# A max-pooling layer's scratch images and group statistics rearranged: one horizontal image, a ring of four pools, statistics on ScalarE

## The chip, the cores and the metric

The kernel runs on one core of a Trainium2 chip. The metric is the device time of one execution in microseconds, as the median of several runs. Five engines work side by side, each with its own in-order instruction queue: TensorE (PE in the profile, its weight loads PEld), VectorE (DVE), ScalarE (ACT), GpSimd (POOL) and SyncE (SP), which here only issues DMAs. They wait for each other through semaphores.

## The reference

The program is four layers applied in turn to two images of 512 channels and 64 x 64 pixels, fp32; each layer adds its result to its input after a group normalization (32 groups of 16 channels). The change is in the third layer, which is a mixture of max pools:

```python
gap = jnp.mean(x, axis=(2, 3))
hmid = jax.nn.relu(jnp.einsum('bc,ec->be', gap, w1) + b1)
score = jnp.einsum('be,ce->bc', hmid, w2) + b2
s = jax.nn.relu(score)
q_s = jnp.clip(jnp.floor(jax.lax.stop_gradient(s)), 0, n_k - 2).astype(jnp.int32)
q_b = q_s + 1
pools = jnp.stack([_maxpool_same(x, k) for k in KERNELS], axis=2)   # KERNELS = 1, 3, 5, 7, 9, 11, 13
...
return frac_b * b_out + frac_s * s_out + x                         # x = x + layer(_gn(x))
```

For each channel, two neighbouring pool sizes are weighted by how far a score lies between two whole numbers. The score comes from the normalized channel means through two small matrices.

## The kernel before, in words

An image lies in SBUF as four chunks of 128 channels (one per partition) x 4096 pixels: `X`, 64 KB per partition. A second buffer of the same size, `Y`, is scratch in this layer. Two such buffers, 128 KB of each partition, live through the whole program.

The layers follow one another. The kernel is written as a data flow, and a framework places each instruction in its engine's queue when the program is built, so that queues don't keep the order of the source: in VectorE's queue the first pooling operations of the third layer stand ahead of the statistics that the source names first. The order is fixed in the built program. Dependent instructions, on one engine or on several, are ordered by semaphores.

The third layer of `Net` (the class that runs; `General` is a fallback behind a condition) has two parts.

`pool_weights` (L1139, calling L637) makes the weights. `self.mv` holds mean and variance per channel, left by the second layer's last step (L1022, L1025). `group_stats` (L75) turns them into group statistics: a small matmul with `self.grp` averages the means over 16 channels (L87), ScalarE negates the result (L89), VectorE centres, squares and adds the channel variances (L92 to L94), a second matmul averages them (L96), VectorE adds the epsilon (L97), and GpSimd raises to the power -1/2 (L99). Then come the normalized means `gap` (L643, L644), two matmuls (L647, L653) with a ReLU between on ScalarE (L650), and some 34 VectorE instructions of 128 x 4 elements (L656 to L680) which make the seven weights per channel `wts`, the factor `c0` of the image itself and the shift `d0`. All of L656 to L665, and the seven triples L670 to L672 that share one tile `t`, depend on each other in turn.

`pool_chunk` (L1140) works on one chunk `cc` of four. A pool of size 2j+1 is made from that of size 2j-1 by a 3 x 3 maximum, horizontal and then vertical. `spread_max` (L683) takes the maximum of the two outer neighbours for all but the edges on VectorE (L692, 3968 elements) and copies the two edge columns or rows on ScalarE (L693). For j = 1 the centre is added by a second maximum each (L1161, L1163). So a chunk has 14 large VectorE operations: 4 for j = 1 and 2 for each of j = 2 to 6. The horizontal results h and the pools p alternate between two images each: h in `Y[:, 0]` and `Y[:, 1]`, p in `Y[:, 2]` and `Y[:, 3]`. Here h1, p1 and so on mean the images of step j.

The weighting is done by TensorE: `add` scales the identity matrix by a column of weights on ScalarE (`dg`, three buffers, L1151) and multiplies each of the eight 512-pixel blocks by it, accumulating in eight PSUM banks (L1153). Seven such sums, of the image and of p1 to p6, make the chunk's result. A pool's image can be overwritten when its sum has read it: p3 takes p1's image, p4 that of p2. ScalarE then moves the eight banks to `X` with the shift (L1183, and L1175 in the last chunk), and statistics for the fourth layer are taken (L1188 to L1196, or L1176 and L1177).

Of the kernel before, what the change touches and what calls it, by code (L numbers as in the profile page):

```python
# [8 lines left out]
F32 = mybir.dt.float32  # L9
I32 = mybir.dt.int32  # L10
AF = mybir.ActivationFunctionType
ALU = mybir.AluOpType
# [3 lines left out]
P = 128  # L16
C = 512
KC = C // P
W = 64
N = W * W  # L20
TB = 512
# [20 lines left out]
def bcast(ap, axis, n):  # L42

    a = ap.unsqueeze(axis)
    shape = list(a.shape)
    shape[axis] = n
    return a.to_broadcast(shape)
# [10 lines left out]
class General:  # L58
# [578 lines left out]
    def pool_weights(self, X, w1, w2, sp, pp, mv=None):  # L637


        nc, vec = self.nc, self.vec  # L640
        nmean, rstd, mv = self.group_stats(X, sp, pp, mv)
        gap = sp.tile([P, KC], F32, name="gap")
        nc.vector.tensor_tensor(gap, mv[:, :, 0], nmean, ALU.add)  # L643
        nc.vector.tensor_tensor(gap, gap, rstd, ALU.mult)  # L644
        ps = pp.tile([P, TB], F32, name="mm")
        for kc in range(KC):
            nc.tensor.matmul(ps[:32, :1], w1[:, kc, :], gap[:, kc:kc + 1], start=(kc == 0),  # L647
                             stop=(kc == KC - 1))
        mid = sp.tile([32, 1], F32, name="mid")
        nc.scalar.activation(mid, ps[:32, :1], AF.Relu, bias=vec[:32, V_B1:V_B1 + 1])  # L650
        ps = pp.tile([P, TB], F32, name="mm")
        for oc in range(KC):
            nc.tensor.matmul(ps[:, oc:oc + 1], w2[:, oc * P:(oc + 1) * P], mid, start=True,  # L653
                             stop=True)
        s, q, t, fb, fs = (sp.tile([P, KC], F32, name=f"pw_{n}") for n in ("s", "q", "t", "fb", "fs"))
        nc.vector.tensor_tensor(s, ps[:, :KC], vec[:, V_B2:V_B2 + KC], ALU.add)  # L656
        nc.vector.tensor_scalar(s, s, 0.0, None, ALU.max)

        nc.vector.tensor_scalar(q, s, 8.0, None, ALU.min)
        qi = sp.tile([P, KC], I32, name="pw_qi")  # L660
        nc.vector.tensor_copy(qi, q)
        nc.vector.tensor_copy(q, qi)
        nc.vector.tensor_tensor(t, q, s, ALU.is_gt)
        nc.vector.tensor_tensor(q, q, t, ALU.subtract)
        nc.vector.tensor_scalar(q, q, 5.0, None, ALU.min)  # L665
        nc.vector.tensor_tensor(fb, s, q, ALU.subtract)
        nc.vector.scalar_tensor_tensor(fs, q, 1.0, s, ALU.add, ALU.subtract)
        wts = sp.tile([P, 7, KC], F32, name="pw_w")
        for j in range(7):
            nc.vector.scalar_tensor_tensor(wts[:, j], q, float(j), fs, ALU.is_equal, ALU.mult)  # L670
            nc.vector.scalar_tensor_tensor(t, q, float(j - 1), fb, ALU.is_equal, ALU.mult)
            nc.vector.tensor_tensor(wts[:, j], wts[:, j], t, ALU.add)  # L672
        c0 = sp.tile([P, KC], F32, name="pw_c0")
        d0 = sp.tile([P, KC], F32, name="pw_d0")
        nc.vector.tensor_tensor(d0, fs, fb, ALU.add)
        nc.vector.scalar_tensor_tensor(d0, d0, 1.0, nmean, ALU.add, ALU.mult)
        nc.vector.tensor_tensor(d0, d0, rstd, ALU.mult)
        nc.vector.tensor_tensor(wts, wts, bcast(rstd, 1, 7), ALU.mult)
        nc.vector.tensor_tensor(c0, wts[:, 0], rstd, ALU.add)
        nc.vector.tensor_scalar(c0, c0, 1.0, None, ALU.add)  # L680
        return c0, d0, wts
# [13 lines left out]
    def pool_chunk(self, X, Y, cc, c0, d0, wts, sp, ppa):  # L695

        nc = self.nc
        x2 = X[:, cc, :]
        img = x2.rearrange("p (y x) -> p y x", x=W)
        tmp = [Y[:, i, :].rearrange("p (y x) -> p y x", x=W) for i in range(KC)]  # L700
        accs = []
        for j in range(1, 7):
            h, p = tmp[j % 2], tmp[2 + j % 2]
            if j == 1:
                self.spread_max(h, img, 2)
                nc.vector.tensor_tensor(h, h, img, ALU.max)
                self.spread_max(p, h, 1)
                nc.vector.tensor_tensor(p, p, h, ALU.max)
                for b in range(NB):
                    xx = x2[:, b * TB:(b + 1) * TB]  # L710
                    nc.scalar.activation(xx, xx, AF.Identity, bias=d0[:, cc:cc + 1],
                                         scale=c0[:, cc:cc + 1])
            else:

                self.spread_max(h, tmp[2 + (j - 1) % 2], 2)
                self.spread_max(p, h, 1)
            dg = sp.tile([P, P], F32, name="dg", bufs=3)
            nc.vector.tensor_scalar(dg, self.ident, wts[:, j, cc:cc + 1], None, ALU.mult)
            p2 = Y[:, 2 + j % 2, :]
            for b in range(NB):  # L720
                if j == 1:
                    acc = ppa.tile([P, TB], F32, name="acc")
                    accs.append(acc)
                nc.tensor.matmul(accs[b], dg, p2[:, b * TB:(b + 1) * TB], start=(j == 1),
                                 stop=(j == 6))
        for b in range(NB):
            xx = x2[:, b * TB:(b + 1) * TB]
            nc.vector.tensor_tensor(xx, xx, accs[b], ALU.add)
# [199 lines left out]
class Net(General):  # L928
# [206 lines left out]
        return w  # L1135

    def pool_weights(self, X, w1, w2, sp, pp):
        return super().pool_weights(X, w1, w2, sp, pp, self.mv)

    def pool_chunk(self, X, Y, cc, c0, d0, wts, sp, ppa):  # L1140


        nc = self.nc
        x2 = X[:, cc, :]
        img = x2.rearrange("p (y x) -> p y x", x=W)
        tmp = [Y[:, i, :].rearrange("p (y x) -> p y x", x=W) for i in range(KC)]
        accs = [ppa.tile([P, TB], F32, name="acc") for b in range(NB)]

        def add(w, src, j):
            dg = sp.tile([P, P], F32, name="dg", bufs=3)  # L1150
            nc.scalar.activation(dg, self.ident, AF.Copy, scale=w)  # L1151
            for b in range(NB):
                nc.tensor.matmul(accs[b], dg, src[:, b * TB:(b + 1) * TB], start=(j == 0),  # L1153
                                 stop=(j == 6))

        add(c0[:, cc:cc + 1], x2, 0)
        for j in range(1, 7):
            h, p = tmp[j % 2], tmp[2 + j % 2]
            if j == 1:
                self.spread_max(h, img, 2)  # L1160
                nc.vector.tensor_tensor(h, h, img, ALU.max)  # L1161
                self.spread_max(p, h, 1)
                nc.vector.tensor_tensor(p, p, h, ALU.max)  # L1163
            else:

                self.spread_max(h, tmp[2 + (j - 1) % 2], 2)
                self.spread_max(p, h, 1)
            add(wts[:, j, cc:cc + 1], Y[:, 2 + j % 2, :], j)
        mv = self.mv[:, cc]
        if cc == KC - 1:  # L1170

            st = sp.tile([P, NB, 6], F32, name="pool_st")
            for b in range(NB):
                xx = x2[:, b * TB:(b + 1) * TB]
                nc.scalar.activation(xx, accs[b], AF.Identity, bias=d0[:, cc:cc + 1])  # L1175
                nc.vector.bn_stats(st[:, b, :], xx)  # L1176
            nc.vector.bn_aggr(mv, st.rearrange("p b s -> p (b s)"))  # L1177
            return
        sums = sp.tile([P, 2, NB], F32, name="pool_sums", bufs=2)
        shift = sp.tile([P, 1], F32, name="pool_shift", bufs=2)  # L1180
        for b in range(NB):
            xx = x2[:, b * TB:(b + 1) * TB]
            nc.scalar.activation(xx, accs[b], AF.Identity, bias=d0[:, cc:cc + 1],  # L1183
                                 accum_out=sums[:, 0, b:b + 1])
            if b == 0:
                nc.scalar.mul(shift, sums[:, 0, 0:1], -1.0 / TB)
            junk = sp.tile([P, TB], F32, name="pool_sq", bufs=2)
            nc.scalar.activation(junk, xx, AF.Square, bias=shift, accum_out=sums[:, 1, b:b + 1])  # L1188
        total = sp.tile([P, 2], F32, name="pool_total", bufs=2)
        nc.vector.tensor_reduce(total, sums, AX.X, ALU.add)  # L1190
        nc.vector.tensor_scalar(total, total, 1.0 / N, None, ALU.mult)
        mean, var = mv[:, 0:1], mv[:, 1:2]
        nc.vector.tensor_copy(mean, total[:, 0:1])
        nc.vector.tensor_tensor(shift, shift, mean, ALU.add)
        nc.vector.tensor_tensor(shift, shift, shift, ALU.mult)
        nc.vector.tensor_tensor(var, total[:, 1:2], shift, ALU.subtract)  # L1196
# [1187 lines left out]
```

## Time and profile before

| | us |
|---|---|
| median of 3 runs | 5740.13 (5734.53 to 5741.96) |
| the profiled execution, its own time | 5741.67 |
| its span, from the first to the last instruction | 5739.9 |
| mean granted TensorE clock | 0.963 |
| TensorE busy | 5451.3 (95%) |
| VectorE busy | 3020.0 (53%) |
| ScalarE busy | 1496.6 (26%) |
| GpSimd busy | 2032.2 (35%) |
| third layer, first image: first L692 to last channel statistics (L1177) | 1693.69 to 1975.16 |
| third layer, second image: first L692 | 4540.70 |

A line of a group gives the source line, engine, operation, the names of what it writes and reads, the shape, and after the bar the busy time in us, the mean of one in ns, the idle time ahead of it and what ended it. A line of the timeline gives start and duration in us, then engine, line, operation and shape, and in brackets the idle time of that engine just before, with the instruction that ended it. A line of waits gives who waited for whom, the us in total, how often, and the longest. Ends of matmuls and spans on POOL are approximate.

### The profile page before, as it was taken

The numbers are of one execution on the slowest core, as the hardware profiler recorded it, in microseconds if no ns is written. First come the engines' busy times: TensorE is split into PE (matmuls) and PEld (weight loads), VectorE is DVE, ScalarE is ACT, GpSimd is POOL, SyncE is SP. The second block draws the span as 40 slices with busy tenths as digits, with TensorE's granted clock in tenths as the row PEclk, the third lists the DMA queues.
The fourth block names the chain that finished last, engine by engine and source line by source line (L and its number), as shares of the span: only waits on it lengthen the run. The fifth ranks groups of instructions, "written<-read, shape, count | busy, mean of one in ns | idle before, by whom it ended". The sixth has DMA issues, their size and how long they took to land.

```text
span 5739.9 us, 52308 instructions
## 1 busy us (share of the span) xinstructions
PE 5451.3 (95%) x20443; PEld 2351.5 (41%) x20443; DVE 3020.0 (53%) x3408; ACT 1496.6 (26%) x2837; POOL 2032.2 (35%) x1518
## 2 busy tenths in 40 slices
PE   7899999999988899999998999999999788999999
PEld 4333333455333344544343333334553234445443
DVE  3245655644678733554432555566456696334444
ACT  1233333114212233222212333330242122332221
POOL 0145666510320045443401565664002200454443
PEclk9899999999998999999998999999999899999999
DMA  3000001100000000101010000011000000000000
GB/s 138 0 10 15 13 15 34 59 24 8 16 1 0 1 1 1 74 15 37 30 54 2 8 15 17 15 34 55 24 24 1 1 0 1 1 1 16 21 15 23
DMA packets 52435, 118.15 MB, mean 21 GB/s; under 512 B 4882, under 2 KB 17938, under 8 KB 50132
## 3 DMA queue, kind: packets, MB, share of 16 engines
q1 hardware_dynamic: 52180, 114.72, 5.7%
q8 instruction: 163, 2.67, 0.2%
q14 instruction: 92, 0.75, 0.0%
HBM read 74.86 MB, written 39.85 MB: 20 GB/s over the span
## 4 chain that ended last, share of the span: by engine, by line
PE 66%; DVE 9%; issue 3%; ACT 1%; POOL 1%; DMA 0%; DVEq 0%; ACTq 0%; POOLq 0%; SPq 0%
PE mm L133 19%; DVE big L692 6%; PE mm L1330 4%; PE mm L1615 4%; PE mm L1370 4%; PE mm L547 4%; PE mm L1932 2%; PE mm L1226 2%; PE mm L1410 2%; PE psO L1242 2%; PE psO L1602 2%; PE mm L2203 2%; PE mm L1631 2%; PE mm L2129 1%; PE tap L2097 1%
## 5 line engine op out<-in xcount | busy, mean ns | idle before, releaser
L133 PE MATMUL mm<-big,w 128*128 128x512 f32 x2560 | 1203.6, 615 | 0.0
L2214 POOL TENSOR_TENSOR late<-late,big 128x512 f32<-128x512 f32 x576 | 718.9, 1282 | 374.9 <-DVE big L2209 374.9
L133 PEld LDWEIGHTS mm<-big,w 128*128 128x128 f32 x2560 | 471.5, 194 | 699.0 <-issue 636.5
L1153 PE MATMUL acc<-big,dg 128*128 128x512 f32 x896 | 407.7, 614 | 79.3 <-DVE big L692 51.1
L2209 DVE TENSOR_TENSOR big<-big,mm 128x512 f32<-128x512 f32 x576 | 364.1, 682 | 194.7 <-PE mm L2203 178.0
L692 DVE TENSOR_TENSOR big<-big 128x3968 f32<-128x3968 f32 x96 | 410.8, 4289 | 38.2 <-PE acc L1153 32.7
L1232 POOL TENSOR_TENSOR total<-prob 128x512 f32<-128x512 f32 x128 | 159.8, 1270 | 761.1 <-ACT prob L1229 761.1
L1584 POOL TENSOR_SCALAR qf_sum<-qf,ksum_ratio 128x512 f32<-128x512 f32 x128 | 199.1, 1565 | 552.1 <-ACT qf L1634 351.5
L1405 POOL TENSOR_TENSOR big<-big 128x512 f32<-128x512 f32 x224 | 278.0, 1273 | 234.9 <-ACT big L1396 234.9
L1609 DVE RECIPROCAL k<-psD 128x512 f32<-128x512 f32 x64 | 214.9, 3358 | 185.0 <-PE psD L1606 185.0
L1153 PEld LDWEIGHTS acc<-big,dg 128*128 128x128 f32 x896 | 173.9, 197 | 311.6 <-issue 283.4
L2144 POOL TENSOR_TENSOR late<-late 128x512 f32<-128x512 f32 x128 | 160.2, 1273 | 383.4 <-ACT late L2133 360.4
L2203 PE MATMUL mm<-late,tapb 18*128 18x512 f32 x1152 | 278.2, 635 | 4.4 <-DVE big L2209 3.3
L1396 ACT ACTIVATE big<-mm,ed 128x256 f32<-128x256 f32 x512 | 194.4, 490 | 276.6 <-DVE top L1392 248.8
L1330 PE MATMUL mm<-proj,k 64*128 64x256 f32 x2048 | 265.1, 391 | 0.9 <-ACT k L1297 0.9
L1249 DVE RECIPROCAL recip<-psD 128x512 f32<-128x512 f32 x64 | 214.9, 3358 | 87.1 <-PE psD L1246 87.1
L1330 PEld LDWEIGHTS mm<-proj,k 64*128 64x128 f32 x2048 | 207.5, 188 | 95.1 <-issue 78.7
L1551 DVE TENSOR_REDUCE tops<-mm 128x2 f32<-128x512 f32 x256 | 159.4, 682 | 163.4 <-PE mm L1330 163.3
L2084 DVE TENSOR_TENSOR prod<-qs,big 128x1024 f32<-128x1024 f32 x192 | 231.0, 1216 | 22.2 <-PE tap L2097 22.2
L133 PE MATMUL mm<-big,big 128*128 128x512 f32 x512 | 239.0, 629 | 0.0
L1615 PE MATMUL mm<-k,w 128*128 128x512 f32 x512 | 235.6, 602 | 0.0
L1370 PE MATMUL mm<-w,big 128*128 128x512 f32 x512 | 234.5, 601 | 0.0
(344 smaller groups left out, 7873.8 us busy)
## 6 DMA issues: line engine op xcount, KB each, us to landing
yd<-late SPq DMA_DIRECT2D x32, 512.0 KB, 2.6
out<-big SPq DMA_DIRECT2D x64, 256.0 KB, 2.0
big<-in_W_kv SPq DMA_DIRECT2D x8, 1024.0 KB, 6.0
big<-yd SPq DMA_DIRECT2D x16, 512.0 KB, 3.7
big<-in_x SPq DMA_DIRECT2D x4, 2048.0 KB, 9.0
big<-in_x SPq DMA_DIRECT2D x6, 1024.0 KB, 12.8
wd<-big SPq DMA_DIRECT2D x6, 1024.0 KB, 4.8
w<-wd SPq DMA_DIRECT2D x24, 256.0 KB, 3.0
```

The source lines that it names most:

```text
L133: self.nc.tensor.matmul(ps, w[:, kc, :], X[:, kc, blk * TB:(blk + 1) * TB], start=(kc == 0), stop=(kc == KC - 1))
L547: nc.tensor.matmul(ps, w[:, kc, oc * P:(oc + 1) * P], att[:, kc, :], start=(kc == 0), stop=(kc == KC - 1))
L692: nc.vector.tensor_tensor(o, a, b, ALU.max)
L1153: nc.tensor.matmul(accs[b], dg, src[:, b * TB:(b + 1) * TB], start=(j == 0), stop=(j == 6))
L1330: nc.tensor.matmul(pS[h][i][:, t, :], k[lo:lo + HD, tok:tok + P], proj[lo:lo + HD, :], start=True, stop=True)
L1370: nc.tensor.matmul(ps, X[:, kc, lo:lo + P], wv[:, kc, :], start=(kc == 0), stop=(kc == KC - 1))
L1405: nc.gpsimd.tensor_tensor(a, a, part, ALU.add)
L1615: nc.tensor.matmul(ps, self.wo[:, kc, oc * P:(oc + 1) * P], qs[:, kc, :], start=(kc == 0), stop=(kc == KC - 1))
L2084: self.nc.vector.tensor_tensor(self.prods[k % 3].rearrange("p (y x) -> p y x", x=W), qs, self.kx[:, y + dy:y + dy + self.UY, dx:dx + W], A ...
L2203: nc.tensor.matmul(ps, self.tapb[32 * q:32 * q + 18, kk, :], el[32 * q:32 * q + 18, :], start=True, stop=True)
L2209: nc.vector.tensor_tensor(dst[:, j * TB:(j + 1) * TB].rearrange("p (y x) -> p y x", x=W), self.vx[:, y:y + self.UY // 2, dx:dx + W], ps.re ...
L2214: nc.gpsimd.tensor_tensor(o, o, dst[:, j * TB:(j + 1) * TB], ALU.add)
```

## The change

1. `pool_weights` of `Net` no longer calls `group_stats`. The centring, squaring, variances, the epsilon and the normalized means are ScalarE instructions; where an operand differs by column, one per column. The two matmuls and GpSimd's power stay; a small GpSimd memset makes the epsilon.
2. What follows the normalized means moves, unchanged, into `pool_mixture`.
3. `pool_chunk` has one horizontal image, `Y[:, 0]`, and a ring of four pools: `Y[:, 1]` to `Y[:, 3]` and a new tile `pool4` of 16 KB per partition. The ring runs on from chunk to chunk: pool number 6 cc + j takes place (6 cc + j) mod 4.

```diff
@@ General.pool_weights
         gap = sp.tile([P, KC], F32, name="gap")
         nc.vector.tensor_tensor(gap, mv[:, :, 0], nmean, ALU.add)
         nc.vector.tensor_tensor(gap, gap, rstd, ALU.mult)
+        return self.pool_mixture(gap, nmean, rstd, w1, w2, sp, pp)
+
+    def pool_mixture(self, gap, nmean, rstd, w1, w2, sp, pp):
+
+        nc, vec = self.nc, self.vec
         ps = pp.tile([P, TB], F32, name="mm")
...
     def pool_weights(self, X, w1, w2, sp, pp):
-        return super().pool_weights(X, w1, w2, sp, pp, self.mv)
+
+        nc, mv = self.nc, self.mv
+        nmean, cent, var, rstd, gap = (sp.tile([P, KC], F32, name=f"pool_{n}")
+                                       for n in ("nmean", "cent", "var", "rstd", "gap"))
+        col = lambda a, kc: a[:, kc:kc + 1]
+        eps = sp.tile([P, 1], F32, name="pool_eps")
+        nc.gpsimd.memset(eps, 1e-5)
+        ps = pp.tile([P, TB], F32, name="mm")
+        nc.tensor.matmul(ps[:, :KC], self.grp, mv[:, :, 0], start=True, stop=True)
+        nc.scalar.mul(nmean, ps[:, :KC], -1.0)
+        for kc in range(KC):
+            nc.scalar.activation(col(cent, kc), mv[:, kc, 0:1], AF.Identity, bias=col(nmean, kc))
+        nc.scalar.activation(var, cent, AF.Square)
+        for kc in range(KC):
+            nc.scalar.activation(col(var, kc), col(var, kc), AF.Identity, bias=mv[:, kc, 1:2])
+        ps = pp.tile([P, TB], F32, name="mm")
+        nc.tensor.matmul(ps[:, :KC], self.grp, var, start=True, stop=True)
+        nc.scalar.activation(var, ps[:, :KC], AF.Identity, bias=eps)
+        nc.gpsimd.tensor_tensor(rstd, var, self.mhalf[:, :KC], ALU.pow)
+        for kc in range(KC):
+            nc.scalar.mul(col(gap, kc), col(cent, kc), col(rstd, kc))
+        return self.pool_mixture(gap, nmean, rstd, w1, w2, sp, pp)
...
     def pool_chunk(self, X, Y, cc, c0, d0, wts, sp, ppa):
...
-        tmp = [Y[:, i, :].rearrange("p (y x) -> p y x", x=W) for i in range(KC)]
+        if cc == 0:
+            self.pools = [Y[:, i, :] for i in range(1, KC)] + [sp.tile([P, N], F32, name="pool4")]
+        image = lambda a: a.rearrange("p (y x) -> p y x", x=W)
+        h = image(Y[:, 0, :])
...
-            h, p = tmp[j % 2], tmp[2 + j % 2]
+            flat = self.pools[(6 * cc + j) % KC]
+            p = image(flat)
...
-                self.spread_max(h, tmp[2 + (j - 1) % 2], 2)
+                self.spread_max(h, last, 2)
                 self.spread_max(p, h, 1)
-            add(wts[:, j, cc:cc + 1], Y[:, 2 + j % 2, :], j)
+            last = p
+            add(wts[:, j, cc:cc + 1], flat, j)
```

## The prediction

> **What bounds the kernel now.** I read the page first: TensorE is busy 95% of the span, but the 13th and 14th of its 40 slices have VectorE at 8 and 7 tenths, and the 33rd at 9. These are the third layer, once per image. A table of busy time by stretch fixes it (columns: PE, PEld, DVE, ACT, POOL busy and counts, clock, DMA):
>
> ```profile
> 1689.00:1751.50 62.50, 25.84 (x68) 12.82 (x67) 41.22 (x63) 3.84 (x12) 5.12 (x1) 0.67 0.00 1
> 1786.20:1847.40 61.20, 51.05 (x112) 21.74 (x112) 60.44 (x21) 18.22 (x52) 0.00 (x0) 0.95 0.00 1
> ```
>
> A steady chunk (second line) has VectorE busy 60.44 of 61.20 us and the next chunks repeat it: it can only be made shorter by less VectorE work. The first line, the layer's start, has VectorE busy only 41.22 of 62.50 us, of which some 17 us from 1734 on are empty. So whatever the change is worth is decided in that start. VectorE's waits between 1685 and 1980 say what they are:
>
> ```profile
> DVE big L692 <- PE acc L1153: 16.4, 1, 16.4
> DVE pw_s L656 <- PE mm L653: 2.9, 1, 2.9
> DVE gap L644 <- POOL gn_rstd L99: 0.9, 1, 0.9
> ```
>
> Together 20.2 us per image (second image: 16.27 for the first). The largest is the third pool, p3, waiting until TensorE has read p1 out of the two-pool ring. The timeline of VectorE and POOL there:
>
> ```profile
> 1721.31 0.15 DVE L97 TENSOR_SCALAR gn_var<-mm 128x4 f32<-128x4 f32 x1
> 1721.50 4.29 DVE L692 TENSOR_TENSOR big<-big 128x3968 f32<-128x3968 f32 x1
> 1721.55 5.12 POOL L99 TENSOR_TENSOR gn_rstd<-gn_var,cst 128x4 f32<-128x4 f32 x1 [42.44 <-DVE gn_var L97]
> ...
> 1729.77 0.16 DVE L656 TENSOR_TENSOR pw_s<-mm,vec 128x4 f32<-128x4 f32 x1 [2.90 <-PE mm L653]
> ...
> 1734.88 0.17 DVE L680 TENSOR_SCALAR pw_c<-pw_c 128x4 f32<-128x4 f32 x1
> 1751.47 4.29 DVE L692 TENSOR_TENSOR big<-big 128x3968 f32<-128x3968 f32 x1 [16.42 <-PE acc L1153]
> ```
>
> Seven pooling operations run before the wait (h1 with its maximum, p1 with its maximum, h2, p2, h3); then the weights' chain L656 to L680 runs alone in 5.28 us (1729.77 to 1735.05); then comes TensorE's sum of the image and p1 (L1153, from 1735.54), 16.42 us after the weights.
>
> The last view shows how small dependent operations get into VectorE's queue when pooling work is ready (second chunk):
>
> ```profile
> 1803.71 0.16 DVE L1190 TENSOR_REDUCE pool_total<-pool_sums 128x2 f32<-128x16 f32 x1
> 1803.93 4.29 DVE L692 TENSOR_TENSOR big<-big 128x3968 f32<-128x3968 f32 x1
> 1808.13 0.16 DVE L1191 TENSOR_SCALAR pool_total<-pool_total 128x2 f32<-128x2 f32 x1
> 1808.32 4.29 DVE L692 TENSOR_TENSOR big<-big 128x3968 f32<-128x3968 f32 x1
> 1812.53 0.15 DVE L1193 COPY channels_mv<-pool_total 128x1 f32<-128x1 f32 x1
> ```
>
> One dependent step per 4.3 us operation. L92, L93, L94 and L97 stand in the same pattern in the layer's start. It is free for VectorE (two L692 start 4.40 us apart with a small one between or without), but it stretches the chain of small steps.
>
> [...] L99, the power on 128x4, takes 1.01 to 1.04 us six times and 5.12 us twice, both times beside such an L692, and ends 0.88 us after it. [...] The trace has 0.17 us (L89, 128x4), 0.20 (L1186, 128x1) and 0.25 (L650, with a bias).
>
> **The change part by part.**
>
> Statistics to ScalarE. VectorE loses L92, L643, L93, L94, L97 and L644, six operations of 0.16 us. Five lie in the bubbles between pooling operations and free nothing; L644 stands alone: 0.2 us gained. ScalarE gains 14 small ACTIVATEs (four centred means, a square, four variances, the epsilon, four products), at about 0.2 us 2.8 us on an engine that is busy 3.84 us of that stretch: covered by idle time, and if not, 2.8 us. A POOL memset of 128x1 comes too, under the 0.53 us of L1503's 128x512, on an idle engine. The chain becomes shorter, because its steps no longer wait for a slot behind a pooling operation: means at 1704.97 (L89), nine ACTIVATEs to about 1706.8, TensorE 0.6, epsilon 0.25, POOL from about 1707.8.
>
> There POOL meets VectorE's back-to-back operations, which before shows only once for the power, followed by idle time. Lower bound: POOL gets in when the running operation ends, at about 1708.2, and holds the next (L1163) back by its 0.9 us. Upper bound: it gets in only when VectorE idles at L656, costing 0.9 us plus what follows to L656: four products 0.8 and 2.84 us (L647 at 1726.93 to L656 at 1729.77), 4.5 us. Where POOL L1405 and VectorE L105 were both queued, around 2323, the four L105 took 3.71 us against 0.48 us each alone, and the four L1405 5.40 against 1.27 each: they took turns. I take 0.9. L656 can then start at about 1712.8, inside L1163's delayed run.
>
> Ring of four. p3 and p4 no longer wait for TensorE; the first pool that does is p5, which needs p1's sum. So p3, h4, p4 and h5 move ahead of the wait, 17.6 us of work (1751.47 to 1769.11 in the chain of waits). But they also stand ready while the weights' chain runs, and by the pattern above each takes a slot between two of its steps. From L656 to h5 six or seven steps fit (L656, L657, L659, L661, L662, L663); the other 20-odd, dependent one by one, run behind h5. The six save 6 x 0.2 = 1.2 us of VectorE time, but weights are complete only after h5, at about 1748 instead of 1735. TensorE's 16.42 us start then, with nothing left to cover them: the wait moves from p3 to p5 and keeps its size.
>
> One horizontal image. h(j+1) is written after p(j) has read h(j): same engine, in order. h(j+1) reads p(j) with its edges in any case, so no new wait arises inside a chunk. At a chunk's turn ScalarE's edge copy of the next h1 has to wait for p6, where it ran ahead before (1773.49): it has 4.29 us, needs 0.45. Bounds 0 to 0.2 us at six turns; I take 0.
>
> pool4 is 16 KB per partition, no DMA; its first write, by p3, falls over 20 us after the second layer's last instruction. After p5 TensorE adds in 7.11 us per pool, VectorE makes one in 8.8: TensorE is about 14 us behind after the first chunk (p5, p6 waiting in the ring), and gets back some 10 us per chunk, so the end of the last chunk (p6, then 7.1 us of sums) stays as it is.
>
> Sum, from the first L692 (1693.69) to p5 (1769.11): 75.42 us, of it 20.23 waiting and 55.19 working. After: 55.19 - 0.2 (L644) - 1.2 (steps in bubbles) + 0.9 (POOL) + 16.4 = 71.1. Gain 4.3 us per image, 8.6 in all; the layers after start that much earlier. The profiled execution has 5739.9 us span and 5741.67 us of its own time, 1.5 us above the median of 5740.13: 5733.1 against 5741.67, or 5731.5 against the median.
>
> **Rivals.**
>
> Chain undivided: if L656 to L680 run together as before (5.28 us from 1713.6), the sums end near 1736, before h5; all 20.2 us go, less 0.9, plus 0.2: 19.5 per image, 39 in all, 5701. For it: L656 to L680 did run so. Against: nothing else was ready then. Between: part of the chain together, 6 to 15 us per image, 5710 to 5728.
>
> POOL shut out: 4.5 instead of 0.9 us, gain 0.7 per image, 5739. For it: in 1721.55 to 1726.67 POOL waited for all of L692. Against: the turns at 2323.
>
> Slower: ScalarE's queue. It is in order, and dg of pool n waits until TensorE has finished pool n-3 (ACT waited 49.8 us for that in this layer of the first image). With TensorE further behind, a dg ahead of an edge copy would hold the next pooling operation: dg of p5, for instance, waits for p2's sum, 7.1 us after p5 begins, while p5 takes 4.29 and the copy 0.3 to 0.45; VectorE loses about 3.2 us. Two such per image outweigh the 4.3; four give 12.8 - 4.3 = 8.5 per image, 5757. Against: before, VectorE lost nothing to ScalarE in this way.
>
> That the ring does nothing isn't a case: p3's wait has no other cause.
>
> **How the numbers follow.** A measurement can tell about 0.2%, 11.5 us, from no change. The forecast has 0.53, of which I give 0.06 to a gain just over 11.5 us; POOL shut out 0.19; undivided 0.12; between 0.06; slower 0.10, half of it within 5750. Faster 0.24, same 0.66, slower 0.10. 5720 to 5750 leaves out the undivided case, most of the between, and half of the slower one: 0.2.
>
> **What would show it.** Right: no wait before p3; a wait of about 16 us for L1153 four operations later; small steps L656 to L663 one by one between L692s; the rest together after h5; a POOL power of 1 to 1.5 us beside a lengthened pooling operation. Wrong: L656 to L680 together early (undivided), an idle VectorE of 4 us before L656 (shut out), or VectorE waiting for L693 behind dg (slower).

## The result: 0.31% slower, and the profile after

| | before | after |
|---|---|---|
| median, us | 5740.4 | 5757.51 (5750.95 to 5763.3) |
| ratio, with its 95% interval | | 1.0031 (1.0014 to 1.0049) |
| the profiled execution, its own time, us | 5741.67 | 5763.3 |
| its span, us | 5739.9 | 5761.2 |
| third layer, first large operation to last channel statistics, us | 281.5 and 281.3 | 286.9 and 286.8 |

The forecast was 5731.5, in a range of 5720 to 5750. The new kernel run once more beside the experiments gave 5754.71, ratio 1.0026 (1.0018 to 1.0033), and again 286.9 and 286.7 us for the layer. So 10.9 us of the loss lie in the layer, some 6 outside it.

Line numbers in the changed kernel are five higher around the pooling helper (L692 is now L697, L693 is L698, L656 is L661, L680 is L685) and some 30 higher further down (L1153 is L1182, L1163 is L1193, L1183 is L1214, L1188 is L1219, L1191 is L1222).

The table of stretches, layer start and a steady chunk (columns as before: PE, PEld, DVE, ACT, POOL busy and counts, clock, DMA):

```profile
1690.50:1753.00 62.50, 10.09 (x35) 5.98 (x33) 57.14 (x60) 6.86 (x26) 1.12 (x2) 0.57 0.02 3
1815.50:1877.00 61.50, 53.92 (x120) 22.84 (x119) 60.42 (x22) 18.51 (x53) 0.00 (x0) 0.97 0.00 0
```

VectorE now works through the start (57.14 of 62.50 us), and TensorE, which had 25.84 us of work there, has 10.09. The steady chunk is as it was. VectorE's waits between 1685 and 1990:

```profile
DVE big L697 <- PE acc L1182: 16.7, 1, 16.7
DVE pw_s L661 <- PE mm L658: 4.4, 1, 4.4
DVE pool_total L1221 <- ACT pool_sq L1219: 4.3, 1, 4.3
```

25.4 us, where before had 20.2. The first is the old wait, at p5 instead of p3. The second is longer than before (2.9), the third is new. The timeline of VectorE at the first and second:

```profile
1705.41 4.22 DVE L697 TENSOR_TENSOR big<-big 128x3968 f32<-128x3968 f32 x1
1714.07 0.16 DVE L661 TENSOR_TENSOR pw_s<-mm,vec 128x4 f32<-128x4 f32 x1 [4.43 <-PE mm L658]
1714.17 4.42 DVE L1193 TENSOR_TENSOR big<-big 128x4096 f32<-128x4096 f32 x1
1718.51 0.16 DVE L662 TENSOR_SCALAR pw_s<-pw_s 128x4 f32<-128x4 f32 x1
1718.63 4.29 DVE L697 TENSOR_TENSOR big<-big 128x3968 f32<-128x3968 f32 x1
1722.84 0.16 DVE L664 TENSOR_SCALAR pw_q<-pw_s 128x4 f32<-128x4 f32 x1
...
1752.73 0.17 DVE L685 TENSOR_SCALAR pw_c<-pw_c 128x4 f32<-128x4 f32 x1
1769.64 17.51 DVE L697 TENSOR_TENSOR big<-big 128x3968 f32<-128x3968 f32 x4 [16.75 <-PE acc L1182]
```

L661 stands in the queue between p1's first part (1705.41) and its second maximum, L1193. It isn't ready; the maximum is, and stands behind it for 4.43 us. GpSimd does not cause this wait: its power starts 0.09 us after ScalarE has its input ready (1709.20 and 0.26 us), and takes its usual time:

```profile
1709.55 1.02 POOL L1161 TENSOR_TENSOR pool_rstd<-pool_var,cst 128x4 f32<-128x4 f32 x1 [3.76 <-ACT pool_var L1160]
```

From then on one step of the weights follows each 4.3 us operation (L662, L664 and so on to L670), and the rest ends at 1752.90. TensorE's first sum starts at 1753.38, 58.25 us after the layer's first operation, where before had 41.84.

VectorE and ScalarE at the third wait, in the second chunk:

```profile
1800.64 4.29 DVE L697 TENSOR_TENSOR big<-pool 128x3968 f32<-128x3968 f32 x1
1809.26 0.17 DVE L1221 TENSOR_REDUCE pool_total<-pool_sums 128x2 f32<-128x16 f32 x1 [4.32 <-ACT pool_sq L1219]
...
1809.56 4.29 DVE L697 TENSOR_TENSOR big<-big 128x3968 f32<-128x3968 f32 x1
```

```profile
1797.90 0.69 ACT L1214 ACTIVATE big<-acc,pw_d 128x512 f32<-128x512 f32 x1 [0.46 <-PE acc L1182]
...
1809.01 0.21 ACT L1219 ACTIVATION_READ_ACCUMULATOR pool_sq<-big,pool_shift 128x1 f32 x1
1809.10 0.42 ACT L698 COPY big<-pool 128x128 f32<-128x128 f32 x1
```

ScalarE moves the first chunk's result out of PSUM and squares it for the statistics (this stretch is called the evacuation below) without a pause from 1797.90 to 1809.22. The edge copy of h2 (L698) stands behind it in order, and p2, which reads those edges, starts at 1809.56, 4.5 us later than the usual 4.4 us after h2. The bracket on L1221 names ScalarE's last square, because a small reduction stands ahead of p2; whether that or the copy is the cause needs an experiment.

Outside the layer, every engine's queue holds the same instructions in the same order in both kernels. What differs is the clock at the seam between the images, first before, then after:

```profile
2889.00:2930.00 41.00, 38.20 (x128) 20.82 (x128) 14.90 (x37) 6.96 (x10) 1.04 (x1) 0.92 0.41 147
2930.00:2980.00 50.00, 50.00 (x162) 26.34 (x162) 11.96 (x26) 7.56 (x11) 0.49 (x2) 0.93 0.00 1
```

```profile
2895.00:2941.00 46.00, 43.20 (x131) 24.71 (x132) 14.89 (x37) 6.95 (x10) 1.04 (x1) 0.81 0.38 132
2941.00:2992.00 51.00, 51.00 (x150) 27.25 (x150) 10.74 (x23) 6.88 (x10) 0.48 (x2) 0.83 0.00 0
```

The second windows don't hold quite the same work: over the same 162 matmuls after (2940.67 to 2995.81) the clock was 0.85, and over the same 128 in the first 0.81. The whole stretch of TensorE's queue from its 9000th matmul (L1330 of before) to its 10700th (L1867 of before) takes 477.5 us before and 484.0 after, again in both. What is left of the span without the two layers and this stretch is 4699.6 us before, and 4703.5 and 4695.5 in the two executions of after: it differs by 8 us between two executions of one kernel.

### The profile page after: what moved, and what is told of

Its sections match the earlier page's. It is cut to its first block, busy times and chain, and to the rows that moved or that the text cites. A ratio compares the mean times of both kernels' runs of the same rounds, so it can differ in the third digit from the quotient of the medians.

```text
span 5761.2 us, 52350 instructions
## 1 busy us (share of the span) xinstructions
PE 5456.3 (95%) x20443; PEld 2357.4 (41%) x20443; DVE 3018.5 (52%) x3396; ACT 1502.2 (26%) x2865; POOL 2024.5 (35%) x1520
## 5 line engine op out<-in xcount | busy, mean ns | idle before, releaser
L1182 PE MATMUL acc<-big,dg 128*128 128x512 f32 x704 | 316.2, 606 | 111.7 <-ACT dg L1180 78.8
L697 DVE TENSOR_TENSOR big<-big 128x3968 f32<-128x3968 f32 x72 | 308.8, 4289 | 38.4 <-PE acc L1182 33.5
L1182 PEld LDWEIGHTS acc<-big,dg 128*128 128x128 f32 x704 | 134.6, 194 | 291.1 <-issue 197.2
```

The costliest lines, as they stand in the source:

```text
L697: nc.vector.tensor_tensor(o, a, b, ALU.max)
```

## The experiments

Theory after the result: (1) the loss begins with the order in VectorE's queue, where the steps of the weights stand one by one between pooling operations, so that TensorE begins late; (2) the late TensorE makes ScalarE's evacuation late, and edge copies stand behind it; (3) the single horizontal image costs some tenths per operation at each chunk's turn. Rivals: the statistics on ScalarE are the cost; the reduction, not the edge copy, holds VectorE in the second chunk; the time at the seam comes of the layer being longer.

### The statistics alone

After, with the four images of before:

```diff
-            flat = self.pools[(6 * cc + j) % KC]
-            p = image(flat)
+            h, p = tmp[j % 2], tmp[2 + j % 2]
+            flat = Y[:, 2 + j % 2, :]
```

> Only the statistics by ScalarE; two horizontal images and two pools as before the change. Theory (the loss comes from the images: the weights' small steps are split up by pooling operations that the ring makes ready, TensorE's sums start later, ScalarE's evacuation of the first chunk then holds an edge copy by 4.5 us, and each turn of a chunk loses 0.6 us): the third pool still waits, the weights are complete some 41 us after the first pooling operation as before, no turn and no evacuation is lost; third layer 281 us per image as before (after the change 287), total 5740, ratio to before 1.000. Rival (the ScalarE statistics cost the time, by the 4.4 us that VectorE waits at the first step of the weights): third layer 285 to 287 us per image, total 5750 to 5757.

5736.01 us, ratio 0.9995 (0.9987 to 1.0004); layer 281.1 and 281.0. The wait at L661 is there (4.3), the wait for TensorE stays at p3 (16.6):

```profile
DVE big L697 <- PE acc L1179: 16.6, 1, 16.6
...
DVE pw_s L661 <- PE mm L658: 4.3, 1, 4.3
```

Alone, the statistics on ScalarE cost nothing: the layer is 0.3 to 0.4 us shorter, and TensorE begins 41.34 us after the layer's first operation instead of 41.84. The wait at L661 (4.3) only stands in place of the two waits of before at L644 and L656 (0.9 and 2.9).

### The images alone

After, with `pool_weights` of before.

```diff
     def pool_weights(self, X, w1, w2, sp, pp):
-        nc, mv = self.nc, self.mv
-        ...
+        return super().pool_weights(X, w1, w2, sp, pp, self.mv)
```

> Only the one horizontal image and the ring of four pools; the statistics on VectorE as before the change. Theory: fifth pool 72 us after the first pooling operation (before 75.4, after the change 74.5), since VectorE does not wait 4.4 us at the weights' first step but interleaves; then 4.5 us lost behind ScalarE's evacuation of the first chunk and 0.6 us at each of three turns: third layer about 284.5 us per image, total about 5747, ratio 1.001. Rival (the statistics by ScalarE cost the time): third layer at most 281 us, total at most 5740.

5750.6 us, ratio 1.0019 (1.0011 to 1.0027); layer 283.8 and 283.7. The wait stands at p5 (16.3 us) and the 4.3 us wait of the second chunk is there:

```profile
DVE big L697 <- PE acc L1161: 16.3, 1, 16.3
DVE pool_total L1200 <- ACT pool_sq L1198: 4.3, 1, 4.3
```

But L661, which here stands behind p3, no longer waits:

```profile
1727.70 4.29 DVE L697 TENSOR_TENSOR pool<-big 128x3968 f32<-128x3968 f32 x1
1731.91 0.15 DVE L661 TENSOR_TENSOR pw_s<-mm,vec 128x4 f32<-128x4 f32 x1
```

The time from the layer's first operation to p5 is 71.47 us, 3.95 less than before and 3.04 less than after. So the images alone cost 2.4 us per image (-3.95, the 4.5 of the second chunk, 1.8 at the turns, for which see the next run). The remaining 3.0 us of the 5.4 come only when the statistics on ScalarE are added to the images: with their shorter chain L661 stands ahead of p1's second maximum, which gives 4.0 us more of waiting and 0.9 us less of work up to p5. The rival, that the statistics cost the time, is wrong for the statistics alone, and right for more than half of the layer's loss in the whole change.

### A second horizontal image added

```diff
+            self.flat_h = [Y[:, 0, :], sp.tile([P, N], F32, name="h2")]
...
-            p = image(flat)
+            p, h = image(flat), image(self.flat_h[(j + 1) % 2])
```

> The changed kernel with a second horizontal image (a new tile of 16 KB per partition), used in turn, and the ring of four. Theory: at a turn of chunks the next chunk's first horizontal maximum can again stand between two dependent operations; three turns of 0.6 us per image come back, the rest stays: third layer 285 us per image against 287, total 3.6 us below the changed kernel, about 5754. Rival (the 0.2 us steps at the turns come from elsewhere, for instance from the ring running on over the turns): no difference, 5757.

5749.77 us, ratio 1.0018 (1.001 to 1.0025); layer 285.9 and 285.5, so 1.0 to 1.3 us came back of the 1.8. At the first turn the three operations after h6 (the next h1, p6, h1's maximum) start 4.21, 4.20 and 4.20 us apart instead of 4.40 each; but the wait in the second chunk grew from 4.3 to 4.9 us, plus 0.26 behind it.

### The chain together

After, with one order given: h2 of the first chunk stands behind the last step of the weights (L685) in VectorE's queue. Only the order differs; no semaphore is added to h2.

```diff
-                self.spread_max(h, last, 2)
+                if cc == 0 and j == 2:
+                    with self.tc.issue_after(self.mixed):      # L685
+                        self.spread_max(h, last, 2)
+                else:
+                    self.spread_max(h, last, 2)
```

> The changed kernel with one more edge of order: the second horizontal maximum of the first chunk stands behind the last step of the weights in VectorE's queue, so that the weights' steps are not split up. Theory: weights complete 29 us after the first pooling operation instead of 58, TensorE's sums done before the fifth pool needs them, no wait of 16.7 us, and TensorE no longer so far behind that ScalarE's evacuation holds an edge copy: 19 to 20 us less per image than the changed kernel, third layer about 267 us, total about 5718, ratio to before 0.996. Rival (the order of VectorE's small steps does not matter, TensorE's sums are late for another reason): fifth pool still waits about 16 us, total within 5 us of 5757.

5706.76 us, ratio 0.9944 (0.993 to 0.9958), against before; layer 267.2 and 267.3. VectorE's timeline:

```profile
1708.98 0.16 DVE L661 TENSOR_TENSOR pw_s<-mm,vec 128x4 f32<-128x4 f32 x1 [4.42 <-PE mm L658]
1709.09 4.43 DVE L1193 TENSOR_TENSOR big<-big 128x4096 f32<-128x4096 f32 x1
1713.43 0.16 DVE L662 TENSOR_SCALAR pw_s<-pw_s 128x4 f32<-128x4 f32 x1
1713.63 0.17 DVE L664 TENSOR_SCALAR pw_q<-pw_s 128x4 f32<-128x4 f32 x1
...
1718.43 0.17 DVE L685 TENSOR_SCALAR pw_c<-pw_c 128x4 f32<-128x4 f32 x1
1718.51 4.28 DVE L697 TENSOR_TENSOR big<-big 128x3968 f32<-128x3968 f32 x1
```

L662 to L685 run in 5.2 us and TensorE starts 29.04 us after the layer's first operation instead of 58.25. Both the 16.7 us wait and the 4.3 us wait of the second chunk are gone; only 4.4 us at L661 stay. The sum holds: 16.75 + 4.4, less the seven steps that stood free in bubbles (7 x 0.2), gives 19.7, and 286.9 - 267.2 is 19.7. Against before it is 14.3 us per image: the 20.2 us of waits, less the 4.4 left and 1.8 at the turns, make 14.0. One line of order decides the sign of the change, and this version is faster than both kernels. Of the 34.3 us that its median lies under that of before, 28.3 are in the two layers; the rest is outside and as open as the 6 us that after loses there.

### The chain together, with the old images

The same order on the first experiment (ScalarE's statistics, two horizontal images, two pools).

> Statistics by ScalarE and the weights' steps kept together ahead of the second horizontal maximum, but with two horizontal images and two pools as before the change. Theory (the gain comes from the weights being early; the ring adds little): sums of the image and the first pool done about 45.4 us after the first pooling operation, the third pool ready at 41.6, so it waits about 4 us; no loss at the turns: third layer about 269 us per image against 267.2 with the ring, total about 5711. Rival (the ring is what lets the early weights pay): the third pool waits 10 us or more, third layer over 275 us, total over 5722.

5712.52 us, ratio 0.995 (0.9936 to 0.9964); layer 269.7 both times. VectorE waits 4.6 us at p3, for p1's sum, and 4.3 at L661:

```profile
DVE big L697 <- PE acc L1179: 4.6, 1, 4.6
DVE pw_s L661 <- PE mm L658: 4.3, 1, 4.3
```

So of the 14.3 us per image that the best version gains, 11.8 come from the order (0.4 of it from the statistics, which were 281.1 alone) and 2.5 from the new images: they save 4.6 at p3 and pay 1.8 to 2 at the turns. The order and the new images with the statistics left on VectorE were not run.

### Both orders, and a second horizontal image

The chain together, a second horizontal image, and the first step of the weights (L661) put behind p1's second maximum.

```diff
-                nc.vector.tensor_tensor(p, p, h, ALU.max)
+                top = nc.vector.tensor_tensor(p, p, h, ALU.max).ins
+                if cc == 0:      # order alone: L661 behind it
+                    self.tc.add_manual_dep(self.mix, top.name, ...)
```

> The kernel with the weights' steps kept together and the ring of four, with a second horizontal image, and with the first step of the weights placed behind the first pool's second maximum instead of ahead of it. Theory: the wait of 4.4 us at the first step of the weights goes, at the price of GpSimd's power meeting a pooling operation (about 1 us): 3.5 us less; the turns give back 1.2 to 1.8: third layer 262 to 263 us per image against 267.2, total about 5698. Rival (GpSimd is shut out by back-to-back pooling operations until VectorE idles): VectorE waits 4 us or more at the first step of the weights all the same, third layer 265.5 to 266.

5713.19 us, ratio 0.9951 (0.9937 to 0.9964); layer 266.4 and 267.1, where 262 to 263 was expected: a miss. The wait at L661 went, and p5 starts 4.2 us earlier. But the second chunk gives it back, in VectorE's timeline and then ScalarE's:

```profile
1776.15 0.17 DVE L1228 TENSOR_REDUCE pool_total<-pool_sums 128x2 f32<-128x16 f32 x1 [5.19 <-ACT pool_sq L1226]
```

```profile
1775.90 0.22 ACT L1226 ACTIVATION_READ_ACCUMULATOR pool_sq<-big,pool_shift 128x1 f32 x1
1775.99 0.31 ACT L698 COPY pool<-big 128x128 f32<-128x128 f32 x1
```

p1's second maximum, which starts at 1776.43, waits 5.19 us for the end of the evacuation. Both p1's edge copy (done at 1776.30) and the small reduction stand between the two; that the copy alone would be enough is taken from the next run, not tested in this one. This run doesn't tell which of its two additions brings the evacuation in the way; the last one does.

### The reduction moved out of the way

After, with the small steps of the first chunk's statistics (L1221 to L1227) placed behind p3 of the second.

```diff
+                if cc == 1 and j == 3:
+                    with self.tc.issue_after(made):    # p3's maximum
+                        self.later()                   # the steps of chunk 0
```

> The changed kernel, with the first chunk's small statistics steps on VectorE moved behind the second chunk's third pool. Theory (the 4.5 us in the second chunk come from the edge copy of its second horizontal maximum, queued on ScalarE behind the evacuation of the first chunk): the pooling operation behind it starts 4.5 us late as before, third layer 286.9 us. Rival (they come from the reduction that stood in VectorE's queue and waited for the last square): the 4.5 us go, third layer 282.4 us.

5756.38 us (a single run); layer 286.7 and 286.8. VectorE's timeline:

```profile
1793.98 4.29 DVE L697 TENSOR_TENSOR big<-pool 128x3968 f32<-128x3968 f32 x1
1802.88 13.11 DVE L697 TENSOR_TENSOR big<-big 128x3968 f32<-128x3968 f32 x3 [4.61 <-ACT big L698]
```

The wait stays and names the edge copy. The reduction was a bystander; rival rejected.

### After once more

> The changed kernel once more. Theory (about 11 us come from the third layer and the rest of the 17 us from the granted clock, which differs from execution to execution): third layer 286.9 and 286.8 us, the rest of the program within 5 us of what the other kernels show there (5170 to 5183 us), total 5748 to 5757. Rival (the change slows the other layers too, by some 6 to 10 us): the rest of the program again at 5187 us, total 5757 to 5763.

The layer came out the same (286.9 and 286.7), the median 5754.71, the seam 484.0 us as the first time. The rest of the program took 5181.1 us, not the 5187 of the rival.

### Before, with one and with three operations more

The kernel before, with p6's vertical maximum done twice in the second chunk, and in another run in the second, third and fourth; the result of the computation is unchanged.

```diff
                 self.spread_max(p, h, 1)
+                if cc == 1 and j == 6:        # second run: 1 <= cc and j == 6
+                    nc.vector.tensor_tensor(p[:, 1:W - 1], h[:, :W - 2], h[:, 2:], ALU.max)
```

> The kernel before, with one pooling operation done twice (the vertical maximum of p6 in the second chunk, on VectorE; the result is the same). Nothing else differs, in any queue. VectorE bounds that chunk, so the layer takes 4.3 to 4.4 us more per image, 285.8 instead of 281.4: 8.7 us for both. Theory 'the seam follows from the time at which it is reached': where the layer is longer by some us, the end of the fourth layer and the start of the second image get a lower clock, 341.6 and 142.4 us for the two stretches instead of 338.7 and 138.8, so the median rises by 8.7 + 6.5 = 15 us to 5753 to 5755, though nothing of the change is in the kernel. Theory 'the seam follows from the change itself' (its additional tile, its engine assignment): the stretches stay at 338.7 and 138.8, the median rises by 8.7 us to 5747.

> The kernel before, with that operation done twice in the second, third and fourth chunk. The layer takes 13 to 13.2 us more per image, 294.6; 26.3 for both. If the time outside the layer jumps once, as soon as the layer is longer: 5738.5 + 26.3 + 6.5 = 5771. If it grows with the layer's length (half as much again): 5738.5 + 39 = 5778. If it depends on where the seam falls, in a pattern that repeats: anything between 5762 and 5772, with the stretches at the seam somewhere between 474.3 and 484 us together. If the seam has nothing to do with the time: 5765.

One more: 5751.28 us, ratio 1.0025 (1.0015 to 1.0034), layer 287.4 and 287.9, together 12.5 us longer. The operation itself is 4.3 of the 5.9 us in the first image; another 1.4 us are for the evacuation, which the later p6 pushes into the next chunk:

```profile
DVE pool_total L1192 <- ACT pool_sq L1190: 1.4, 1, 1.4
```

The median rose by 11.9. Three more: 5774.45 us, ratio 1.0064 (1.005 to 1.0078), layer 298.4 and 299.1, 34.7 us longer instead of the 26.3 expected, the median 35.1. So a layer that is longer by as much as the change makes it, or by three times that, costs just that much: the stretch at the seam took 477.5 and 473.9 us. The theory that a longer layer brings the low clock there is rejected.

### The chain together, with a second horizontal image

The fourth experiment plus the third one's edit, nothing else.

> The version with the weights' chain together, with the second horizontal image alone added to it (the first step of the weights stays where it was, so VectorE still waits 4.4 us for it). The three turns give back 0.6 us each, 1.8 us per image: layer 265.4 instead of 267.2. If the evacuation on ScalarE takes part of it again, as it did with the first step moved, the wait there is under 2 us, since this version reaches the second chunk some 4 us later: layer 265.4 to 267. Median 5703 to 5707, plus up to 6 if the seam has the lower clock, as it had with both orders changed.

5723.76 us, ratio 0.9971 (0.996 to 0.9982); layer 270.9 and 271.6: a miss. The turns did give back 1.8 us, but a wait of 5.5 us behind the evacuation came:

```profile
DVE pool_total L1225 <- ACT pool_sq L1223: 5.5, 1, 5.5
```

267.2 - 1.8 + 5.5 is the 270.9. The reason is order again. With two horizontal images the next chunk's h1 stands ahead of p6 in VectorE's queue, so p6 starts 72.04 us after the layer's first operation instead of 68.07, and the evacuation runs from 78.6 to 90.5 instead of from 73.6 to 85.0. p1's edge copy stands behind it in both; p1's first part ends at 85.7 there and at 85.1 here, so there the copy is made in time and here it is 5.5 us late. (The small reduction waits for the same evacuation here. That the copy holds p1's second maximum by itself is carried over from the run that moved the reduction; this run doesn't test it.) The single image forces p6 first. What costs 0.6 us at a turn saves 5.5 us here.

### The seam, over all runs

| | layer, first image | seam, us | median less both layers |
|---|---|---|---|
| before | 281.5 | 477.5 | 5176 to 5178 |
| after; once more | 286.9; 286.9 | 484.0; 484.0 | 5183.8; 5181.1 |
| images alone; second horizontal image; reduction moved | 283.8; 285.9; 286.7 | 484.0; 484.1; 484.0 | 5183.1; 5178.4; 5182.9 |
| both orders; together with second image | 266.4; 270.9 | 484.0; 484.0 | 5179.7; 5181.3 |
| statistics alone | 281.1 | 481.2 | 5173.9 |
| together; together, old images | 267.2; 269.7 | 474.3; 474.5 | 5172.3; 5173.1 |
| one more; three more | 287.4; 298.4 | 477.5; 473.9 | 5176.0; 5177.0 |

The seam is from one profiled execution of each kernel (two of after), the last column from the medians. The seam takes one of a few values. The time outside the layer is 5178 to 5184 us with 484, and 5172 to 5178 with 474 to 481; within these groups it doesn't follow the seam (5173.9 with 481.2, but 5177.0 with 473.9). The 6.5 us between 477.5 and 484.0 are the size of what is missing outside the layer, so I put it there; that is a coincidence of sizes over these runs, not a test. What chooses the value stays open: neither the layer's length (last row) nor the ring by itself (it is in "together", which has 474.3) decides it.

## Why the prediction was wrong, step by step

**The ring moves the wait and keeps its size: right.** No wait stands before p3; four operations later stands one of 16.75 us (16.4 foretold). The steps of the weights took one bubble each between L697s (L662, then L664 and L666 to L670, seven and not six), the rest ran behind h5. The weights were complete 57.8 us after the layer's first operation, where the forecast's 1748 is 54.3. The whole sign hangs on this splitting: with the chain put together by one order, the layer is 19.7 us shorter than with it split. The rival "chain undivided" (19.5 per image against before) named the right mechanism; its size came to 14.3, since the wait at L661 and the turns, both taken near nothing, stay.

**"L656 can then start inside L1163's delayed run": the step that failed first.** It was costed at nothing, and L661 waits 4.43 us. The bound of 4.5 us was for POOL being shut out; POOL wasn't: its power took 1.02 us, almost all in VectorE's idle time. So the sign named for that rival, an idle VectorE of 4 us before L656, appeared without its cause. What held VectorE was its own queue: L661 stands ahead of a ready L1193, and with L661 behind it (the run with both orders) the wait is gone. ScalarE keeps the order of its queue in the same way: the edge copy runs at 1809.10, behind the last instruction of the evacuation (1809.01), though p1, which it reads, was complete at 1800.60 (L1193, 4.42 us from 1796.18), and p2 loses 4.5 us by it. The start (first operation to p5) became 0.9 us shorter, 74.51 against 75.42, not 4.3: waits 21.2 instead of 16.4, work 53.3 instead of 54.7. With the images alone, where L661 doesn't wait, it is 71.47. That this lies near the foretold 71.1 is luck, since the forecast was for the change as a whole. The forecast priced the statistics and the ring one by one; that the first changes the place of L661 among the operations of the second, worth 3.0 us per image, was no term of it.

**The turns, taken as 0, with a bound of 0.2 each:** 0.2 us at three operations of each of three turns, 0.6 a turn and so beyond the bound, 1.8 us per image. Before, the next h1 stood between h6 and p6, and an operation that needs nothing from the one ahead of it starts 4.20 us after it, a dependent one 4.40. With one horizontal image each depends on the last. Undoing that part gives the 4.20 back.

**"The end of the last chunk stays as it is": right for the end, but 4.5 us per image are lost on the way to it.** At the end itself VectorE waits 3.2 us for ScalarE, where before had 3.1. The second chunk, which the sum takes as unchanged, loses the 4.5. That TensorE is behind was seen; that it starts ScalarE's evacuation late, in the way of an edge copy, was not. The rival "slower" had this queue with another instruction at its head, the scaled identity (dg) instead of the evacuation, and ended at 5757; that the measured 5757.51 meets this number is a coincidence, since its sum has other terms. The reduction's removal shows the edge copy to be what VectorE waits for, and the second horizontal image, added to the version with the chain together, that the time of the evacuation decides.

**The sum, per image:** -0.9 + 4.5 + 1.8 = 5.4 us, and the layer went from 281.5 to 286.9.

**Outside the layer** the forecast took the time as fixed. It rose by some 6 us, with the clock at the seam; that term was missing. Where it lies is inferred from sizes, and its cause is open.

**Statistics on ScalarE, POOL's power, dg:** the first is worth 0.4 us per image by itself and costs 3.0 beside the ring. The 0.9 us for the power, estimated from the 0.88 us by which L99 outlasts L692 in before, was too high: with L661 behind the maximum, the power started first and L1193 beside it took its usual 4.42. Of a dg that holds an edge copy, the rival "slower" in its own form, VectorE's list of waits shows nothing.

## What to carry to other kernels

Before pricing a new buffer, read where the small dependent steps that gate the next engine stand in the in-order queue: more buffers make more work ready, and ready work put between those steps delays the engine that they feed (here TensorE starts 58.25 us after the layer's first operation instead of 29.04). Taking away a wait moves the time of everything behind it, so list what each other engine has in order behind its longest uninterrupted stretch (here 11 us of evacuation) and ask whether a short operation that somebody waits for now lands behind it. A spare buffer and a forced order are not independent: the single scratch image cost 0.6 us at a turn and, by putting p6 first, avoided a wait of 5.5.

## What the runs showed of the hardware that was not expected

A power on POOL and a VectorE operation with both inputs in SBUF can overlap (0.82 us here), at least as the spans are recorded (those on POOL are rough). In the run with both orders, POOL's and VectorE's timelines:

```profile
1704.52 1.02 POOL L1161 TENSOR_TENSOR pool_rstd<-pool_var,cst 128x4 f32<-128x4 f32 x1 [3.75 <-ACT pool_var L1160]
```

```profile
1704.72 4.42 DVE L1193 TENSOR_TENSOR big<-big 128x4096 f32<-128x4096 f32 x1
```

POOL began 0.20 us earlier and neither was lengthened (1.02 and 4.42 us are what they take alone). In the kernel before, the power began 0.05 us after a VectorE operation (L99 at 1721.55, L692 at 1721.50) and took 5.12 us; this order of the two shows no such cost. What makes the difference was not shown.

A pooling operation that depends on the one just ahead of it costs VectorE 0.2 us more than one that doesn't: at the first turn two of 4.29 us start 4.40 us apart in the changed kernel and 4.20 to 4.21 us apart with a second horizontal image. For these large maxima a wait for the operation just ahead does cost time, and it is what the turns cost.

The clock that TensorE is granted at one and the same stretch of work differs between kernels: 0.92 and 0.93 over two runs of 128 and 162 matmuls at the seam of before, 0.81 and 0.85 over the same matmuls of after, with the same instructions in all queues there. The whole stretch took 477.5 us in before and 484.0 in both profiled executions of after.
